# An adapter and expert-FFN kernel: the start of the first adapter, the expert bias fold and the last output stage rearranged

## The chip, the core and the metric

The kernel runs on one core of one Trainium2 chip. A core has five engines that run their own instruction streams side by side and wait for each other through semaphores: TensorE (PE, matrix products into the PSUM memory; its weight loads are listed as PEld), VectorE (DVE), ScalarE (ACT), GpSimd (POOL) and SyncE (SP, which here only issues transfers). Data moves between the device's memory and the on-chip SBUF by 16 DMA engines. The metric is the time of one execution on the device in microseconds; lower is better.

## What is computed

The input x is 2 sequences of 2048 tokens with 512 features, all in 32-bit floats. Two layers follow one another. The first is an adapter with an expert chosen per sequence by `itok_B_0_15`, the second a feed-forward network (FFN) with an expert chosen per sequence by `itok_B_0_7`:

```python
# layer 0: A = 128, 16 experts
hidden = gelu(x @ down_W.T + down_b)
expert_out = hidden @ expert_W[idx].T + expert_b[idx]
domain_output = where(valid, expert_out, hidden)
hidden = domain_output + domain_emb[idx]
hidden = hidden @ up_W.T + up_b
x = layernorm(hidden + x, eps=1e-5) * ln_gamma + ln_beta
# layer 1: I = 2048, 8 experts
h = gelu(x @ Wi[e] + bi[e])
o = h @ Wo[e] + bo[e]
out = layernorm(o + x, eps=1e-12) * gamma[e] + beta[e]
```

## The kernel before

The 4096 tokens are handled as eight blocks of 512 (`TB`), four to a sequence. A block is four subtiles of 128 tokens by 512 features; `x_tiles[n]` holds block n and is changed in place until it is stored. The order of all instructions is written out by hand: each engine runs its instructions in the order in which the program states them, and waits where an operand or a buffer isn't ready.

The loop over n at the end of the program runs `f_in(n)` (the FFN's first matrix with its gelu) and then `f_out(n)` (its second matrix). Both use a Strassen-like scheme that needs seven block products for eight, with sums of weight blocks made by GpSimd (`sums_wi`, `sums_wo`) and sums of activations by VectorE. Products go through `product` (L380) and are called pX, pY, pZ, pW in the first stage and gX, gY, gZ, gW in the second, after their PSUM banks. Other small work is hung between the products by hooks: the adapter of block n + 1 sits in the hooks of `f_out(n)`, the final layernorm of block n - 1 in those of `f_in(n)`, and the loads of later weights too.

For block 0 there is no FFN to hide the adapter in, so it is written out ahead of the loop (L645 to L699), and this is what most of the change touches. Its steps are these.

- `keep_busy(k)` issues k products of a matrix of ones that nobody reads, into the bank called idle. Each 32-bit product shows as two records in the profile.
- `a_transpose(0, s)` transposes subtile s of x on TensorE (pt_x, four pieces) and ScalarE copies it to SBUF as xT. For block 0 the banks are the two of `ps_z`. The matrices down_W and up_W are transposed in the same way and copied by VectorE (dWT, uWT).
- The product pflags spreads the two flags (expert valid or not) over 128 partitions.
- `a_down(0, s, s + 1)` is the down projection of one subtile (pdown), followed by ScalarE's gelu into hid. In block 0 all four use the single bank of `ps_w`.
- `fold_expert` lets VectorE mix the expert's matrix with the identity by the flag (eff), and makes the expert's bias plus the domain embedding into a column, which it spreads to a 128 x 128 tile (biasx). `fold_up` multiplies eff with uWT (pw), and ScalarE copies the result (up): expert and up projection become one matrix.
- `a_up(0, s)` is the up projection of a subtile (pup): hid times up, then `add_bias`, which is biasx times uWT and a one-row product of ones with up_b. VectorE adds the result to x and takes mean and variance; GpSimd makes the inverse deviation (rstd).
- `a_norm(0, s)` normalizes on VectorE in two instructions (L279, L280), `a_out(0, s)` transposes the result for the FFN (pt_y), with ScalarE's copy to yT. `fold_bi` transposes the FFN's first bias.

For the other blocks `fold_bias` makes the whole bias of the up projection once for a sequence (pb, copied by ScalarE to the sequence's upb), and `a_residual(n)` lets GpSimd add it to x ahead of the up projection. The folds of the second sequence are hooked into `f_in(3)`.

Small PSUM tiles come from `aux`, a pool of two banks (`ps_a`) taken in turns: a third tile waits until the first is read.

Transfers at the start go out on two queues. ScalarE issues down_W, two subtiles of x, down_b, up_W, up_b, and the layernorm rows broadcast to 128 partitions (g, b). SyncE issues the token indices, two subtiles of x, and then, when the expert's number has been loaded into a register, the expert's matrix (ew), its bias and the domain embedding as columns (eb), and the FFN's weights.

The last block's `f_out_last` has no hooks. Its two last product pairs are split by subtile (q = 0, 1), Y and V of each in banks of their own; VectorE adds them to x, and the four subtiles are normalized and stored, 2 and 3 first.

Of the kernel before, what the change touches and what calls it, by code (L numbers as in the profile page):

```python
# [9 lines left out]
F32 = mybir.dt.float32  # L10
# [7 lines left out]
def kernel(  # L18
# [34 lines left out]
    P = 128  # L53
# [32 lines left out]
    def aux(name, pool=None, tag="aux"):  # L86
        return (pool or ps_a).tile([P, 512], F32, tag=tag, name=name)
# [24 lines left out]
    db = cpool.tile([A, 1], F32, name="db")  # L112
    g0 = cpool.tile([P, D], F32, name="g0")
    b0 = cpool.tile([P, D], F32, name="b0")
    upb = cpool.tile([1, D], F32, name="upb")
    nc.sync.dma_start(x_tiles[0][:, 0, :], xr[0][:, 0, :])
    nc.scalar.dma_start(dW, down_W)
    nc.sync.dma_start(x_tiles[0][:, 1, :], xr[0][:, 1, :])
# [1 line left out]
    nc.scalar.dma_start(x_tiles[0][:, 3, :], xr[0][:, 3, :])  # L120
    nc.scalar.dma_start(db, down_b.rearrange("(a o) -> a o", o=1))
    nc.scalar.dma_start(uW, up_W.rearrange("(c p) a -> p c a", p=P))
    nc.scalar.dma_start(upb, up_b.rearrange("(o d) -> o d", o=1))
    nc.scalar.dma_start(g0, ln_gamma.partition_broadcast(P))
    nc.scalar.dma_start(b0, ln_beta.partition_broadcast(P))

# [28 lines left out]

    def load_expert(b):
        w = seq[b]
        w["ew"] = spool.tile([A, A], F32, tag="ew", name=f"ew_{b}")
        nc.sync.dma_start(w["ew"], expert_W[ds(e0[b], 1)].rearrange("e o a -> (e o) a"))
        w["eb"] = spool.tile([A, 2], F32, tag="eb", name=f"eb_{b}")  # L160
        nc.sync.dma_start(w["eb"][:, 0:1], expert_b[ds(e0[b], 1)].rearrange("e o -> o e"))
        nc.sync.dma_start(w["eb"][:, 1:2], domain_emb[ds(e0[b], 1)].rearrange("e o -> o e"))

    def load_bi(b):
        w = seq[b]
# [8 lines left out]
    def fold_expert(b):  # L174

        w = seq[b]
        v, iv = flags_all[:, 0, b : b + 1], flags_all[:, 1, b : b + 1]

        eff = spool.tile([A, A], F32, tag="eff", name=f"eff_{b}")
        nc.vector.tensor_scalar(eff, ident, iv, None, ALU.mult)  # L180
        nc.vector.scalar_tensor_tensor(eff, w["ew"], v, eff, ALU.mult, ALU.add)
        bias = spool.tile([A, 1], F32, tag="ebias", name=f"ebias_{b}")
        nc.vector.scalar_tensor_tensor(bias, w["eb"][:, 0:1], v, w["eb"][:, 1:2], ALU.mult, ALU.add)
        biasx = spool.tile([A, P], F32, tag="biasx", name=f"biasx_{b}")
        nc.vector.tensor_scalar(biasx, ones, bias, None, ALU.mult)
        w["biasx"], w["eff"] = biasx, eff

    def fold_up(b):
        w = seq[b]
# [2 lines left out]
        w["up"] = spool.tile([A, D], F32, tag="up", name=f"up_{b}")  # L192
        nc.scalar.copy(w["up"], pw)

    def fold_bias(b):
        w = seq[b]
        pb = aux(f"pb_{b}")
        add_bias(pb, w, True)
        w["upb"] = spool.tile([P, D], F32, tag="upb", name=f"upb_{b}")
        nc.scalar.copy(w["upb"], pb)  # L200

    def add_bias(bank, w, start):

        nc.tensor.matmul(bank, w["biasx"], uWT, start=start, stop=False)
        nc.tensor.matmul(bank, ones[0:1, :], upb, start=False, stop=True)  # L205

    def fold_bi(b):
        w = seq[b]
# [91 lines left out]
    def a_down(n, lo, hi):  # L300

        xT = live["xT"]
        if lo == 0:
            live["hid"] = t_pool.tile([A, TB], F32, tag="hid", name=f"hid_{n}")
        t = slice(lo * P, hi * P)
        ph = aux(f"pdown_{n}_{lo}", ps_w, "W") if n == 0 else aux(f"pdown_{n}")
        for c in range(NC):
            nc.tensor.matmul(ph[:, t], dWT[:, c, :], xT[:, c, t], start=(c == 0), stop=(c == NC - 1))  # L308
        nc.scalar.activation(live["hid"][:, t], ph[:, t], AF.Gelu, bias=db, scale=1.0)

    def a_residual(n):

        for s in range(NS):
            nc.gpsimd.tensor_tensor(x_tiles[n][:, s, :], x_tiles[n][:, s, :], seq[n // BPB]["upb"], ALU.add)

    def a_up(n, s):
        w = seq[n // BPB]
        pu = aux(f"pup_{n}_{s}")
        nc.tensor.matmul(pu, live["hid"][:, ts(s, P)], w["up"], start=True, stop=(n > 0))  # L319
        if n == 0:  # L320
            add_bias(pu, w, False)
        r = x_tiles[n][:, s, :]
        nc.vector.tensor_add(r, pu, r)
        if s == 0:
            live["mv"] = moments_tile(f"a_{n}")
        moments(live["mv"], s, r, f"a_{n}_{s}")
        if n == 0:
            live["rstd", s] = rstds(live["mv"], s, s + 1, EPS0, f"a_{n}_{s}")
        elif s % 2:
            live["rstd", s] = live["rstd", s - 1] = rstds(live["mv"], s - 1, s + 1, EPS0, f"a_{n}_{s}")  # L330
# [181 lines left out]
    def f_out(n, hooks, last):  # L512
# [27 lines left out]
        def f_out_last(n, add):  # L540

            X, Z, W = bank(ps_x, "X"), bank(ps_z, "Z"), bank(ps_w, "W")
            every = range(NP)
            mul(X, a11, w["b11"], early, True)
            h_s13(n, ND - 1)
            h_s2(n, 0)
            h_s2(n, 1)
            mul(X, a11, w["b11"], late, False)
            add(r11, X)
            mul(Z, "s1", w["t1"], every, True)  # L550
            h_s4(n, 0)
            h_s4(n, 1)
            add(r22, Z)
            add(r12, Z)
            mul(X, "s2", w["t2"], every, False)
            add(r12, X)
            mul(X, s3, w["t3"], every, False)
            add(r21, X)
            add(r22, X)
            mul(W, a22, w["t4"], every, True)  # L560
            add(r21, W)
            for s in (2, 3):
                f_moments(n, s)
            f_rstd(n, 2, 4)
            for q in range(2):
                Y, V = (bank(ps_y, "Y"), bank(ps_z, "Z")) if q == 0 else (bank(ps_a, "aux"), bank(ps_a, "aux"))
                mul(Y, a12, w["b21"], every, True, (q,))
                mul(V, "s4", w["b22"], every, True, (q,))
                f_normalize(n, 2 + q)
                f_store(n, 2 + q)  # L570
                add(r11[:, q], Y[:, q])
                add(r12[:, q], V[:, q])
                f_moments(n, q)
                f_rstd(n, q, q + 1)
            for q in range(2):
                f_normalize(n, q)
                f_store(n, q)

        if last:
            f_out_last(n, add)  # L580
# [77 lines left out]
        for _ in range(k):  # L658
            nc.tensor.matmul(idle[:, :P], ones, ones, start=True, stop=True, skip_group_check=True)  # L659

    idle = aux("idle", ps_y, "Y")
    dWT = cpool.tile([P, NC, A], F32, name="dWT")
    uWT = cpool.tile([A, D], F32, name="uWT")
    flags_all = cpool.tile([P, 2, B], F32, name="flags_all")
    keep_busy(24)
    a_transpose(0, 0)
    pd = aux("pt_dW")
    for c in range(NC):
        nc.tensor.transpose(pd[:, ts(c, P)], dW[:, ts(c, P)], ident)
    nc.vector.tensor_copy(dWT.rearrange("p c a -> p (c a)"), pd)  # L670
    a_transpose(0, 1)
    pf = aux("pflags")
    nc.tensor.matmul(pf[:, : 2 * B], ones[0:1, :], flags.rearrange("o f b -> o (f b)"), start=True, stop=True)
    nc.vector.tensor_copy(flags_all.rearrange("p f b -> p (f b)"), pf[:, : 2 * B])
    a_transpose(0, 2)
    a_down(0, 0, 1)
    a_transpose(0, 3)
    pu = aux("pt_uW")
    for c in range(NC):
        nc.tensor.transpose(pu[:, ts(c, P)], uW[:, c, :], ident)  # L680
    nc.vector.tensor_copy(uWT, pu)
    for s in range(1, NS):
        a_down(0, s, s + 1)
    keep_busy(4)
    fold_expert(0)
    fold_up(0)
    a_up(0, 0)
    a_up(0, 1)
    keep_busy(8)
    a_norm(0, 0)  # L690
    fold_bi(0)
    a_norm(0, 1)
# [92 lines left out]
```

## Time and profile before

| what | us |
|---|---|
| median of three runs (lowest, highest) | 903.06 (902.8, 903.95) |
| the profiled execution | 903.51 |
| its span in the profile | 901.7 |

The profile covers one execution. Its span is 1.8 us shorter than that execution's time. A look at the stretches of the span gives this (busy microseconds of each engine):

| stretch, us | what runs | PE | DVE | ACT | POOL | DMA share |
|---|---|---|---|---|---|---|
| 1.06 to 9.36 | idle products | 8.30 | 1.22 | 1.17 | 0.31 | 0.75 |
| 9.36 to 23.19 | transposes, down projections, fold, first up projection | 12.24 | 2.50 | 4.40 | 0.00 | 1.06 |
| 23.19 to 36.35 | other up projections, layernorm | 12.29 | 10.04 | 1.17 | 2.27 | 0.93 |
| 36.35 to 54.21 | first FFN products of block 0 | 17.33 | 10.00 | 4.07 | 17.70 | 0.00 |
| 54.21 to 414.47 | blocks 0 to 2 and the first FFN stage of block 3 | 360.26 | 195.16 | 100.14 | 144.53 | 0.19 |
| 475 to 880 | blocks 4 to 7 | 403.09 | 220.77 | 106.23 | 147.96 | 0.19 |
| 894.1 to 901.7 | after the last product | 0.00 | 4.27 | 0.00 | 0.99 | 0.18 |

A busy TensorE is not a TensorE doing useful work: the idle products count as busy. A line of the timeline reads: start in us, length in us, engine, line, operation, output and input by the program's names, shapes, how many instructions are merged, and in brackets how long the engine stood idle before it and what released it. The chain of waits lists the work that ended last, followed back from the end.

### The profile page before, as it was taken

Reading aid. Unit: us, or ns where it says so; the run is one execution under the profiler, and the core shown is the slowest. Engines: PE = TensorE matmul, PEld = TensorE weight load, DVE = VectorE, ACT = ScalarE, POOL = GpSimd, SP = SyncE. Lnnn points to the kernel's source line nnn. Section 1 sums busy time; section 2 is a strip of 40 time slices with the busy share of each in tenths; the row PEclk is TensorE's granted clock in tenths of the full one; section 3 lists DMA queues with packets and bytes.
Section 4 is the critical chain, followed back from the end, with each engine's and each line's share of the span. In section 5 each row is a group of like instructions: output and inputs, shape, how many; then the busy total and the mean of one; then the engine's idle time right before and its main releaser. Section 6 shows DMA issues by size and latency. Waiting matters only on the chain.

```text
span 901.7 us, 10542 instructions
## 1 busy us (share of the span) xinstructions
PE 888.1 (98%) x4112; PEld 751.3 (83%) x4112; DVE 484.0 (54%) x691; ACT 225.1 (25%) x461; POOL 335.0 (37%) x251
## 2 busy tenths in 40 slices
PE   8999999999999999999999999999999999999996
PEld 7588888887888878888788888888888887888875
DVE  1644374743657546563556747464474853556325
ACT  2134201441024301343013520144101440124200
POOL 0498511542214612344026971144411551223001
PEclk9999999999999999999999999999999999999999
DMA  8522100340013300151007610034000440011001
GB/s 287 218 73 71 45 1 1 128 152 1 1 40 134 108 0 1 63 186 48 0 1 257 187 47 1 0 117 155 10 1 1 140 141 1 1 48 45 1 1 47
DMA packets 47286, 62.16 MB, mean 69 GB/s; under 512 B 2917, under 2 KB 36485, under 8 KB 46342
## 3 DMA queue, kind: packets, MB, share of 16 engines
q1 hardware_dynamic: 45844, 59.93, 19.5%
q10 hardware_dynamic: 1394, 1.58, 0.6%
q8 instruction: 32, 0.52, 0.2%
q14 instruction: 16, 0.13, 0.1%
HBM read 53.11 MB, written 8.39 MB: 68 GB/s over the span
## 4 chain that ended last, share of the span: by engine, by line
PE 98%; DVE 1%; ACT 0%; issue 0%; DVEq 0%
PE gX L380 18%; PE pX L380 18%; PE pZ L380 12%; PE gZ L380 12%; PE gW L380 6%; PE pW L380 6%; PE pY L380 6%; PE gY L380 6%; PE pup L319 3%; PE pdown L308 3%; PE pC L380 2%; PE pt_x L292 2%; PE pt_y L292 1%; PE idle L659 1%; PE gaux L380 1%; PE pup L205 0%
## 5 line engine op out<-in xcount | busy, mean ns | idle before, releaser
L400 ACT ACTIVATE h<-c,biT 128x256 f32<-128x256 f32 x248 | 105.7, 497 | 76.1 <-DVE c L447 76.1
L380 PE MATMUL gX<-wo,h 128*128 128x256 f32 x512 | 115.6, 379 | 1.7 <-DVE x L537 1.7
L380 PE MATMUL pX<-yT,wi 128*128 128x256 f32 x496 | 117.2, 379 | 0.0
L380 PEld LDWEIGHTS gX<-wo,h 128*128 128x128 f32 x512 | 95.6, 190 | 14.1 <-DVE x L537 2.1
L380 PEld LDWEIGHTS pX<-yT,wi 128*128 128x128 f32 x496 | 94.2, 190 | 12.8
L443 ACT COPY c<-pX 128x512 f32<-128x512 f32 x93 | 54.0, 581 | 182.4 <-PE pX L380 182.4
L275 POOL TENSOR_TENSOR rstd_a<-ve_a,mhalf 128x2 f32<-128x2 f32 (+1 forms) x18 | 16.0, 888 | 204.1 <-DVE ve_a L273 204.1
L231 POOL TENSOR_TENSOR wis<-wi 128x512 f32<-128x512 f32 x31 | 40.8, 1315 | 129.5 <-PE pZ L380 129.5
L447 DVE TENSOR_TENSOR c<-pX,c 128x512 f32<-128x512 f32 x31 | 21.4, 691 | 111.2 <-ACT c L443 111.2
L293 ACT COPY yT<-pt_y 128x512 f32<-128x512 f32 x32 | 18.7, 587 | 227.9 <-PE pt_y L292 227.9
L537 DVE TENSOR_TENSOR x<-gX,x 128x512 f32<-128x512 f32 x32 | 21.4, 688 | 99.5 <-PE gX L380 99.4
L275 POOL TENSOR_TENSOR rstd_f<-ve_f,mhalf 128x4 f32<-128x4 f32 (+2 forms) x10 | 10.2, 1025 | 155.6 <-DVE ve_f L273 155.6
L504 DVE TENSOR_TENSOR s<-s,h 128x512 f32<-128x512 f32 x32 | 35.7, 1155 | 47.9 <-PE gZ L380 47.9
L343 POOL TENSOR_TENSOR x<-x,bo 128x512 f32<-128x512 f32 x32 | 41.4, 1298 | 53.2 <-PE pt_y L292 53.2
L380 PEld LDWEIGHTS gX<-wos,s 128*128 128x128 f32 x256 | 48.6, 190 | 13.2 <-issue 6.7
L380 PE MATMUL pX<-yTs,wis 128*128 128x256 f32 x248 | 58.7, 379 | 0.0
L380 PEld LDWEIGHTS gZ<-wos,s 128*128 128x128 f32 x256 | 48.6, 190 | 12.1 <-issue 6.2
L380 PE MATMUL pZ<-yT,wis 128*128 128x256 f32 x248 | 58.6, 379 | 0.0
L380 PE MATMUL pZ<-yTs,wis 128*128 128x256 f32 x248 | 58.6, 379 | 0.0
L380 PE MATMUL pY<-yT,wi 128*128 128x256 f32 x248 | 58.6, 379 | 0.0
L380 PE MATMUL pW<-yTs,wi 128*128 128x256 f32 x248 | 58.6, 379 | 0.0
L380 PE MATMUL gX<-wos,s 128*128 128x256 f32 x256 | 57.8, 379 | 0.3 <-DVE x L537 0.3
(114 smaller groups left out, 1544.8 us busy)
## 6 DMA issues: line engine op xcount, KB each, us to landing
wi<-in_L_cond_Wi_dram SPq DMA_DIRECT2D x64, 512.0 KB, 4.4
wo<-in_L_cond_Wo_dram SPq DMA_DIRECT2D x16, 512.0 KB, 10.2
out_dram<-x SPq DMA_DIRECT2D x32, 256.0 KB, 2.0
x<-in_x_dram SPq DMA_DIRECT2D x7, 1024.0 KB, 6.4
x<-in_x_dram SPq DMA_DIRECT2D x2, 256.0 KB, 4.6
x<-in_x_dram ACTq DMA_DIRECT2D x2, 256.0 KB, 4.7
bo<-in_L_cond_bo_dram SPq DMA_DIRECT2D x2, 256.0 KB, 5.3
gamma<-in_L_cond_gamma_dram SPq DMA_DIRECT2D x2, 256.0 KB, 6.8
```

What stands on the lines that cost most here:

```text
L231: tt(s1, a21, a22, ALU.add)
L275: nc.gpsimd.tensor_tensor(rstd[:, lo:hi], ve[:, lo:hi], mhalf[:, lo:hi], ALU.pow)
L292: nc.tensor.transpose(pt[:, ts(c, P)], src[:, ts(c, P)], ident)
L308: nc.tensor.matmul(ph[:, t], dWT[:, c, :], xT[:, c, t], start=(c == 0), stop=(c == NC - 1))
L319: nc.tensor.matmul(pu, live["hid"][:, ts(s, P)], w["up"], start=True, stop=(n > 0))
L343: nc.gpsimd.tensor_tensor(r, r, seq[n // BPB]["bo"], ALU.add)
L380: nc.tensor.matmul(bank[:, q], lhsT(k, q), rhs(k, q), start=first, stop=True, skip_group_check=True)
L400: nc.scalar.activation(h[:, j, c * HT : (c + 1) * HT], pre[:, q], AF.Gelu, bias=w["bi"][:, j : j + 1], scale=1.0)
L443: nc.scalar.copy(t, src)
L447: nc.vector.tensor_add(t, src, t)
L504: nc.vector.tensor_tensor(t[:, i : i + 2], s1[:, i : i + 2], h_blocks(n, k, k + 2)[0], ALU.subtract)
L537: nc.vector.tensor_add(t, src, t)
```

## The change

There are six parts.

1. Idle products: 9 instead of 24 at the start, and none of the 4 and 8 later ones. They use a bank of `ps_x` instead of the one of `ps_y`.
2. Order at the start: flags and down_W's transposes go ahead of the transposes of x; all four transposes of x then go ahead of the down projections. Those alternate between the banks of `ps_w` and `ps_y`. The fold of the expert (`fold_expert`, `fold_up`) moves ahead of the last down projection.
3. The expert's bias: expert_b and domain_emb are loaded as rows, ahead of the expert's matrix. VectorE makes their sum as a row, and a small product of that row with a row of ones (pe) gives biasx, which ScalarE copies out of PSUM. This holds for both sequences.
4. up_b is loaded broadcast to 128 partitions.
5. GpSimd adds it to the four subtiles of block 0 (`a_residual(0)`), and the one-row product with up_b leaves block 0's up projections. `fold_bias` keeps it.
6. In `f_out_last` subtile 0 is normalized and stored between the two last adds, ahead of the add of the last product.

```diff
--- before.py
+++ after.py
@@ -112,7 +112,7 @@
     db = cpool.tile([A, 1], F32, name="db")
     g0 = cpool.tile([P, D], F32, name="g0")
     b0 = cpool.tile([P, D], F32, name="b0")
-    upb = cpool.tile([1, D], F32, name="upb")
+    upb = cpool.tile([P, D], F32, name="upb")
     nc.sync.dma_start(x_tiles[0][:, 0, :], xr[0][:, 0, :])
     nc.scalar.dma_start(dW, down_W)
     nc.sync.dma_start(x_tiles[0][:, 1, :], xr[0][:, 1, :])
@@ -120,7 +120,7 @@
     nc.scalar.dma_start(x_tiles[0][:, 3, :], xr[0][:, 3, :])
     nc.scalar.dma_start(db, down_b.rearrange("(a o) -> a o", o=1))
     nc.scalar.dma_start(uW, up_W.rearrange("(c p) a -> p c a", p=P))
-    nc.scalar.dma_start(upb, up_b.rearrange("(o d) -> o d", o=1))
+    nc.scalar.dma_start(upb, up_b.partition_broadcast(P))
     nc.scalar.dma_start(g0, ln_gamma.partition_broadcast(P))
     nc.scalar.dma_start(b0, ln_beta.partition_broadcast(P))
 
@@ -155,11 +155,11 @@
 
     def load_expert(b):
         w = seq[b]
+        w["eb"] = spool.tile([1, 2, A], F32, tag="eb", name=f"eb_{b}")
+        nc.sync.dma_start(w["eb"][:, 0, :], expert_b[ds(e0[b], 1)])
+        nc.sync.dma_start(w["eb"][:, 1, :], domain_emb[ds(e0[b], 1)])
         w["ew"] = spool.tile([A, A], F32, tag="ew", name=f"ew_{b}")
         nc.sync.dma_start(w["ew"], expert_W[ds(e0[b], 1)].rearrange("e o a -> (e o) a"))
-        w["eb"] = spool.tile([A, 2], F32, tag="eb", name=f"eb_{b}")
-        nc.sync.dma_start(w["eb"][:, 0:1], expert_b[ds(e0[b], 1)].rearrange("e o -> o e"))
-        nc.sync.dma_start(w["eb"][:, 1:2], domain_emb[ds(e0[b], 1)].rearrange("e o -> o e"))
 
     def load_bi(b):
         w = seq[b]
@@ -175,15 +175,13 @@
 
         w = seq[b]
         v, iv = flags_all[:, 0, b : b + 1], flags_all[:, 1, b : b + 1]
+        row = spool.tile([1, A], F32, tag="ebias", name=f"ebias_{b}")
+        nc.vector.scalar_tensor_tensor(row, w["eb"][:, 0, :], flags[:, 0, b : b + 1], w["eb"][:, 1, :], ALU.mult, ALU.add)
 
         eff = spool.tile([A, A], F32, tag="eff", name=f"eff_{b}")
         nc.vector.tensor_scalar(eff, ident, iv, None, ALU.mult)
         nc.vector.scalar_tensor_tensor(eff, w["ew"], v, eff, ALU.mult, ALU.add)
-        bias = spool.tile([A, 1], F32, tag="ebias", name=f"ebias_{b}")
-        nc.vector.scalar_tensor_tensor(bias, w["eb"][:, 0:1], v, w["eb"][:, 1:2], ALU.mult, ALU.add)
-        biasx = spool.tile([A, P], F32, tag="biasx", name=f"biasx_{b}")
-        nc.vector.tensor_scalar(biasx, ones, bias, None, ALU.mult)
-        w["biasx"], w["eff"] = biasx, eff
+        w["ebias"], w["eff"] = row, eff
 
     def fold_up(b):
         w = seq[b]
@@ -192,17 +190,18 @@
         w["up"] = spool.tile([A, D], F32, tag="up", name=f"up_{b}")
         nc.scalar.copy(w["up"], pw)
 
+        pe = aux(f"pe_{b}")
+        nc.tensor.matmul(pe[:, :P], w["ebias"], ones[0:1, :], start=True, stop=True)
+        w["biasx"] = spool.tile([A, P], F32, tag="biasx", name=f"biasx_{b}")
+        nc.scalar.copy(w["biasx"], pe[:, :P])
+
     def fold_bias(b):
         w = seq[b]
         pb = aux(f"pb_{b}")
-        add_bias(pb, w, True)
+        nc.tensor.matmul(pb, w["biasx"], uWT, start=True, stop=False)
+        nc.tensor.matmul(pb, ones[0:1, :], upb[0:1, :], start=False, stop=True)
         w["upb"] = spool.tile([P, D], F32, tag="upb", name=f"upb_{b}")
         nc.scalar.copy(w["upb"], pb)
-
-    def add_bias(bank, w, start):
-
-        nc.tensor.matmul(bank, w["biasx"], uWT, start=start, stop=False)
-        nc.tensor.matmul(bank, ones[0:1, :], upb, start=False, stop=True)
 
     def fold_bi(b):
         w = seq[b]
@@ -303,22 +302,27 @@
         if lo == 0:
             live["hid"] = t_pool.tile([A, TB], F32, tag="hid", name=f"hid_{n}")
         t = slice(lo * P, hi * P)
-        ph = aux(f"pdown_{n}_{lo}", ps_w, "W") if n == 0 else aux(f"pdown_{n}")
+        if n == 0:
+            ph = aux(f"pdown_{n}_{lo}", *((ps_y, "Y") if lo % 2 else (ps_w, "W")))
+        else:
+            ph = aux(f"pdown_{n}")
         for c in range(NC):
             nc.tensor.matmul(ph[:, t], dWT[:, c, :], xT[:, c, t], start=(c == 0), stop=(c == NC - 1))
         nc.scalar.activation(live["hid"][:, t], ph[:, t], AF.Gelu, bias=db, scale=1.0)
 
     def a_residual(n):
 
+
+        by = seq[n // BPB]["upb"] if n else upb
         for s in range(NS):
-            nc.gpsimd.tensor_tensor(x_tiles[n][:, s, :], x_tiles[n][:, s, :], seq[n // BPB]["upb"], ALU.add)
+            nc.gpsimd.tensor_tensor(x_tiles[n][:, s, :], x_tiles[n][:, s, :], by, ALU.add)
 
     def a_up(n, s):
         w = seq[n // BPB]
         pu = aux(f"pup_{n}_{s}")
         nc.tensor.matmul(pu, live["hid"][:, ts(s, P)], w["up"], start=True, stop=(n > 0))
         if n == 0:
-            add_bias(pu, w, False)
+            nc.tensor.matmul(pu, w["biasx"], uWT, start=False, stop=True)
         r = x_tiles[n][:, s, :]
         nc.vector.tensor_add(r, pu, r)
         if s == 0:
@@ -562,19 +566,24 @@
             for s in (2, 3):
                 f_moments(n, s)
             f_rstd(n, 2, 4)
-            for q in range(2):
-                Y, V = (bank(ps_y, "Y"), bank(ps_z, "Z")) if q == 0 else (bank(ps_a, "aux"), bank(ps_a, "aux"))
+            banks = (bank(ps_y, "Y"), bank(ps_z, "Z")), (bank(ps_a, "aux"), bank(ps_a, "aux"))
+            for q, (Y, V) in enumerate(banks):
                 mul(Y, a12, w["b21"], every, True, (q,))
                 mul(V, "s4", w["b22"], every, True, (q,))
-                f_normalize(n, 2 + q)
-                f_store(n, 2 + q)
+
+            def finish(s):
+                f_normalize(n, s)
+                f_store(n, s)
+
+            for q, (Y, V) in enumerate(banks):
+                finish(2 + q)
                 add(r11[:, q], Y[:, q])
+                if q:
+                    finish(0)
                 add(r12[:, q], V[:, q])
                 f_moments(n, q)
                 f_rstd(n, q, q + 1)
-            for q in range(2):
-                f_normalize(n, q)
-                f_store(n, q)
+            finish(1)
 
         if last:
             f_out_last(n, add)
@@ -658,35 +667,33 @@
         for _ in range(k):
             nc.tensor.matmul(idle[:, :P], ones, ones, start=True, stop=True, skip_group_check=True)
 
-    idle = aux("idle", ps_y, "Y")
+    idle = aux("idle", ps_x, "X")
     dWT = cpool.tile([P, NC, A], F32, name="dWT")
     uWT = cpool.tile([A, D], F32, name="uWT")
     flags_all = cpool.tile([P, 2, B], F32, name="flags_all")
-    keep_busy(24)
-    a_transpose(0, 0)
+    keep_busy(9)
+    pf = aux("pflags")
+    nc.tensor.matmul(pf[:, : 2 * B], ones[0:1, :], flags.rearrange("o f b -> o (f b)"), start=True, stop=True)
+    nc.vector.tensor_copy(flags_all.rearrange("p f b -> p (f b)"), pf[:, : 2 * B])
     pd = aux("pt_dW")
     for c in range(NC):
         nc.tensor.transpose(pd[:, ts(c, P)], dW[:, ts(c, P)], ident)
     nc.vector.tensor_copy(dWT.rearrange("p c a -> p (c a)"), pd)
-    a_transpose(0, 1)
-    pf = aux("pflags")
-    nc.tensor.matmul(pf[:, : 2 * B], ones[0:1, :], flags.rearrange("o f b -> o (f b)"), start=True, stop=True)
-    nc.vector.tensor_copy(flags_all.rearrange("p f b -> p (f b)"), pf[:, : 2 * B])
-    a_transpose(0, 2)
+    for s in range(NS):
+        a_transpose(0, s)
+    a_residual(0)
     a_down(0, 0, 1)
-    a_transpose(0, 3)
+    a_down(0, 1, 2)
     pu = aux("pt_uW")
     for c in range(NC):
         nc.tensor.transpose(pu[:, ts(c, P)], uW[:, c, :], ident)
     nc.vector.tensor_copy(uWT, pu)
-    for s in range(1, NS):
-        a_down(0, s, s + 1)
-    keep_busy(4)
+    a_down(0, 2, 3)
     fold_expert(0)
     fold_up(0)
+    a_down(0, 3, 4)
     a_up(0, 0)
     a_up(0, 1)
-    keep_busy(8)
     a_norm(0, 0)
     fold_bi(0)
     a_norm(0, 1)
```

## The prediction

> **What bounds the kernel now.** I read the page first, then the chain of waits in order of time, then the timeline of the first 60 us and of the last 20.
>
> ```profile
> span 901.7 us, 10542 instructions
> PE 888.1 (98%) x4112; PEld 751.3 (83%) x4112; DVE 484.0 (54%) x691; ACT 225.1 (25%) x461; POOL 335.0 (37%) x251
> PE 98%; DVE 1%; ACT 0%; issue 0%; DVEq 0%
> ```
>
> TensorE is busy all the time and carries the chain, so no other engine's work in the middle is worth anything. But "busy" in the first 36 us includes filler. The chain there, piece by piece (start, length, what):
>
> ```profile
> 1.06 8.57 PE idle L659 x48
> ...
> 17.73 0.89 PE idle L659 x8
> 18.62 0.88 PE pw L191 x2
> ...
> 19.52 0.59 ACT up L193
> ...
> 20.16 1.13 PE pup L319 x2
> 21.28 0.86 PE pup L204 x2
> 22.14 1.05 PE pup L205 x2
> 23.19 1.06 PE pup L319 x2
> ...
> 26.16 1.98 PE idle L659 x16
> ```
>
> Idle products hold 8.57 + 0.89 + 1.98 = 11.4 us of chain. Each up projection is three matmuls, about 2.97 us, for four subtiles; the third (L205) multiplies one row of ones by the up bias. At 36.35 the first FFN product (pC) starts, and from there to 880 TensorE hardly waits. Call T the end of the first up projection (23.19); T to pC is 13.16 us.
>
> The end, from the timeline:
>
> ```profile
> 890.64 0.42 DVE L537 TENSOR_TENSOR x<-gaux,x 128x256 f32<-128x256 f32 x1 [0.45 <-PE gaux L380]
> 894.10 0.43 DVE L537 TENSOR_TENSOR x<-gaux,x 128x256 f32<-128x256 f32 x1 [3.03 <-PE gaux L380]
> ...
> 895.50 0.15 DVE L273 TENSOR_SCALAR ve_f<-mv_f 128x1 f32<-128x1 f32 x1
> 895.57 0.74 DVE L279 SCALAR_TENSOR_TENSOR x<-x,mv_f,gamma 128x512 f32<-128x512 f32 x1
> 895.74 0.99 POOL L275 TENSOR_TENSOR rstd_f<-ve_f,mhalf 128x1 f32<-128x1 f32 x1 [5.92 <-DVE ve_f L273]
> 896.42 0.75 DVE L280 SCALAR_TENSOR_TENSOR x<-x,rstd_f,beta 128x512 f32<-128x512 f32 x1
> 897.09 0.74 DVE L279 SCALAR_TENSOR_TENSOR x<-x,mv_f,gamma 128x512 f32<-128x512 f32 x1
> 897.93 0.75 DVE L280 SCALAR_TENSOR_TENSOR x<-x,rstd_f,beta 128x512 f32<-128x512 f32 x1
> ```
>
> VectorE normalizes two subtiles after the last matmul, although the first was ready before a 3.03 us idle.
>
> **What the Trainium skill says.** "TensorE: Matmul & The Clock Gate", What's actually happening: the array starts at half rate and goes to full rate after about 3.4 us of sustained work, counted in a free-running window. The trace agrees in kind: idle products start every 0.213 us until about 6.8 us and every 0.107 after, though it took 5.7 us. "SBUF — State Buffer", Who interferes with whom: a VectorE instruction with two SBUF inputs and a GpSimd one that reads SBUF block each other whole. The trace agrees: the normalize step at L279 takes 0.74 us alone (27.94) and 1.75 at 37.52 beside GpSimd's sums (L231, 1.60 there, 1.27 elsewhere). "TensorEngine Tiling (Array Packing)", Key Properties: a change of tiling mode drains the array. I read the one-row products so: L205 takes 1.05 against 0.86 for L204, and the product after it 1.06 against 0.86, 0.19 us at each edge.
>
> **The change part by part.**
>
> *Start, to the fold.* Nine products instead of 24: 18 records at 0.213 from 1.06 end near 4.9. The flags product (flags ready at 3.71 + 0.16 = 3.87) then waits for nothing: to 5.4. The dW transposes (dW lands at 1.07 + 2.8 = 3.9) take 4 x 0.213: to 6.25; VectorE's copy (0.69) ends at 7.05. x: the second subtile lands at 1.86 + 4.6 = 6.5, the first, issued 0.4 us earlier, near 6.1, the last ACT one at 7.3 (4.7 is the mean of 4.1 and 5.3, issue 2.00). So the transposes of x follow at once, and TensorE works without a gap until about 7: I take the clock to rise at 6.8 as before. They go through two Z banks and ScalarE copies of 0.59, so ScalarE sets the pace: copies end at 7.7, 8.3, 9.0, 9.65, TensorE is through at 8.95. Down projections at 0.89: 0 to 9.8, 1 (now in the Y bank, so it no longer waits for gelu 0) to 10.7, uW transposes 0.44 to 11.1, uWT copied at 11.85, down 2 to 12.0.
>
> The fold on VectorE: row about 0.2 (0.21 for the bias column now), eff 0.28 + 0.35, without hindrance at about 12.65. Its inputs: on SP, ew moves behind two row loads; slots were 6.14, 6.69, 7.21, so ew goes out at 7.2 and, with the 3.8 us it had (the wait of the bi load on ew ended at 10.0), lands at 11.0. The wi, bi and bo loads behind it keep their slots. eb as rows goes out at 6.14 and 6.69; columns landed in 3.5 and 4.9 us, so rows by 10.2 to 11.6 at worst.
>
> Hindrance: GpSimd now adds up_b to the four subtiles. upb grows from 2 KB to 256 KB; its issue stays at 4.95 and g right behind it landed 4.3 us after its own, so I take 9.4. Then four adds of 1.27 to 1.7 us run from 9.4 to about 15, over the fold. Row and the second eff step have two SBUF inputs; each may wait for the rest of one add (0 to 1.27). I take 1.25 in all: eff at 13.9. pw 0.88 to 14.85, up copied (0.59) at 15.45; the new product pe (two records of 128 columns, 0.21, plus 0.19 at its edges) to 15.25, biasx copied (0.37) at 15.8, both beside down 3 (0.89 + 0.19, to 16.35). Up projection 0: 2 x 0.86, so T = 18.05 instead of 23.19: **5.15 saved**. That down 3 now lies behind the fold is what hides the copies; without it they would cost about 0.6.
>
> upb's extra 254 KB take 0.7 us at 348 GB/s (9.36 to 23.19). It delays g (landed 9.8, read at T + 3.6), wi, wo and x1 by as much; wo is first read by GpSimd's sums (L255) at 49. Hidden.
>
> *T to pC.* The one-row products go: 4 x 1.25 (0.86 + two edges) and 1.98 of filler leave TensorE. What is late next is VectorE, in program order after T: up 0 with statistics 1.86, up 1 1.74, two normalizes and the biT copy 3.19 (27.94 to 31.13), up 2 1.9, up 3's add 0.74: T + 9.4, and the last transposes, ScalarE's copy and pC's start 1.38 more (34.97 to 36.35). TensorE fits in between, also with two aux banks (up 3 waits for biT's bank until T + 5.3, ends T + 7.1). pC at T + 10.8: **2.36 saved**. GpSimd's rstd stays hidden behind the other normalize; the residual adds are over by 15, before the first add on VectorE.
>
> *pC to 880.* Nothing goes or comes except, at the second sequence's fold (403), pe: 0.21 + 2 x 0.19: **0.6 lost**, between 0.3 (no edges) and 0.9 (the bias product behind it then waits for the biasx copy; queued behind it are all FFN products). ScalarE would copy biasx at 405.2 to 405.6, and the bias product is due at 406.2, so no wait. VectorE's shorter fold there (0.29 for biasx) was hidden anyway.
>
> *End.* Normalize and store of subtile 0 (1.5 us) go between the two last adds, into the 3.03 us idle: 891.1 to 892.7. SP's stores keep order, one goes earlier. After the last matmul the remaining normalize's second half waits for GpSimd's rstd (895.74 + 0.99), so it starts at 896.8 and ends at 897.55 instead of 898.68: **1.13 saved**. At worst 0.75 if the wait costs more, at best 1.5 with the last store running alone.
>
> Sum: 5.15 + 2.36 - 0.6 + 1.13 = 8.0. Against its own time the profiled execution goes from 903.51 (span 901.7 and 1.8 around it) to 895.5; the median shown is 0.45 lower, so 903.06 becomes **895.0**.
>
> **Rivals.**
>
> *No collision.* The adds fall elsewhere, or the 128-column steps slip between them: 1.25 more, 893.7. For it: the two steps are short. Against it: four adds back to back cover 5.6 us around the fold.
>
> *A later fold.* Each VectorE step waits out a full add (up to 2.5), or ew or the eb rows land 1 to 2 us later because upb shares the DMA engines, whose share was already 0.97 to 1.08 between 3 and 7 us; or the clock rises one window (3.4 us) later, which costs the down projections 0.9 each. About 2.5 lost: 897.5. Against it: 3 us lie between ew's landing and its use.
>
> *Cold array (slower).* With the filler gone, TensorE has gaps before x and between banks, and no window counts as busy until the FFN starts. Then records double: down 0 to 2 2.7, x transposes 0.65, uW, pw, pe and down 3 2.6, up 0 1.72, so 7.7 to T; the stage after T becomes TensorE's, 2.3; pC's first windows 2.6. That is 12.6: 907.6. It decides once the array stays at half rate past T (7.7 plus some of the 2.3 eats the 8.0). Against it: TensorE is gapless to about 7 us and some 80% busy to the fold; gaps after it are about 1 us.
>
> **How the numbers follow.** The forecast's own range is 893.8 to 896.8; chance 0.50. No collision 0.19, later fold 0.24, cold 0.05; 0.02 for no change, which only a partly cold array could make. Range 892.8 to 898.2: below it a better end, above it the cold case and part of the later fold. Faster by over 0.2% (1.8 us, about what a measurement of this kernel can tell) 0.93, same 0.02, slower 0.05.
>
> **What would show it.** T near 18 and pC near 29; idle records spaced 0.213 until the flags product and transposes at 0.107 from about 7; GpSimd's adds between 9 and 15 and VectorE's eff step lengthened beside them; the VectorE-bound stretch of 10.8 after T; the product behind pe lengthened by 0.19 near 395; the last VectorE step starting right after GpSimd's rstd. The prediction is wrong if 512-column records show about 0.85 instead of 0.43 before pC, if the eff step ends after 16, or if pC waits for wi.

## The result and the profile after

| | median, us | lowest to highest | runs |
|---|---|---|---|
| before | 903.06 | 902.65 to 904.04 | 7 |
| changed | 899.22 | 895.56 to 902.11 | 7 |

The ratio is 0.9948 with a 95% interval of 0.9926 to 0.9971. The change gains 3.8 us, about half a per cent, where 8.0 were forecast, and its runs spread over 6.5 us where those of before spread over 1.4. The profiled execution is the slowest of the seven, 902.11, only 1.40 below that of before. The page of the changed kernel (span; busy time of the engines; chain by engine):

```profile
span 900.3 us, 10433 instructions
PE 883.6 (98%) x4054; PEld 747.2 (83%) x4054; DVE 485.0 (54%) x689; ACT 225.3 (25%) x463; POOL 339.7 (38%) x255
PE 94%; DVE 1%; issue 1%; ACT 0%; POOLq 0%; POOL 0%; DVEq 0%; ACTq 0%
```

TensorE has 58 records fewer, but only 4.5 us less busy time; part of what was taken away came back as slower products. The timeline shows where it begins:

```profile
12.01 5.09 POOL L318 TENSOR_TENSOR x<-x,upb 128x512 f32<-128x512 f32 x4 [10.64 <-DMA eb<-n_L_cond_domain_emb_dram]
...
12.85 0.57 DVE L179 SCALAR_TENSOR_TENSOR ebias<-eb,flags 1x128 f32<-1x128 f32 x1
...
13.35 1.34 DVE L182 TENSOR_SCALAR eff<-ident,flags_all 128x128 f32<-128x128 f32 x1
14.73 1.25 DVE L183 SCALAR_TENSOR_TENSOR eff<-ew,flags_all,eff 128x128 f32<-128x128 f32 x1
...
16.04 1.12 PE L189 MATMUL pw<-uWT,eff 128*128 128x512 f32 x2 [2.94 <-DVE eff L183]
...
19.67 1.92 PE L323 MATMUL pup<-up,hid 128*128 128x512 f32 x2
```

The label in brackets names the load of eb; upb itself landed at 11.9 (issued at 5.49, 6.4 us to landing). GpSimd's four adds lie over the fold on VectorE, whose two eff steps take 1.34 and 1.25 us. In the kernel before:

```profile
14.25 0.28 DVE L180 TENSOR_SCALAR eff<-ident,flags_all 128x128 f32<-128x128 f32 x1
...
14.56 0.35 DVE L181 SCALAR_TENSOR_TENSOR eff<-ew,flags_all,eff 128x128 f32<-128x128 f32 x1
```

TensorE stands idle 2.94 us for eff, and the first up projection's pair of records then takes 1.92 us against 1.13 before. The same in a table by stretches (length; busy time and number of instructions of PE, PEld, DVE, ACT, POOL; granted TensorE clock; DMA share; GB/s):

```profile
13.00:16.00 3.00, 0.10 (x1) 0.00 (x0) 2.95 (x3) 0.37 (x1) 3.00 (x4) 1.00 1.09 360
...
17.00:24.00 7.00, 7.00 (x17) 4.10 (x17) 0.60 (x1) 1.22 (x3) 0.10 (x1) 0.51 1.08 362
...
34.00:38.00 4.00, 4.00 (x12) 3.21 (x12) 3.79 (x4) 0.00 (x0) 3.92 (x3) 0.57 0.67 259
```

The third number from the end is the one to see: after three microseconds with almost no matmul TensorE runs at half rate for seven, and once more at the start of the FFN. The kernel before in the same stretches:

```profile
13.00:16.00 3.00, 2.54 (x22) 2.27 (x20) 1.65 (x5) 1.09 (x3) 0.00 (x0) 1.00 1.10 356
...
17.00:24.00 7.00, 6.33 (x25) 3.11 (x24) 0.73 (x2) 0.95 (x2) 0.00 (x0) 1.00 1.07 375
...
34.00:38.00 4.00, 3.13 (x17) 2.31 (x17) 3.52 (x7) 1.17 (x2) 1.83 (x2) 1.00 0.25 96
```

(The column reads 1.00 in the first microseconds too, where the idle records are spaced 0.213 us; it does not show that slow start.) The seven timed runs, each with its mean granted clock, follow the same order:

| us | 895.56 | 895.60 | 898.45 | 899.22 | 899.63 | 899.74 | 902.11 |
|---|---|---|---|---|---|---|---|
| clock | 0.999 | 0.999 | 0.997 | 0.997 | 0.997 | 0.995 | 0.993 |

One stretch of 3.4 us at half rate takes 1.7 of 900 us from the mean clock, 0.002; the profiled run had three such lengths (6.83 from 17.14 on and 3.42 from 34.20). The clock also falls behind the last product, where nothing is left for TensorE to do (from 897.8 on here, from 898.1 in the kernel before). How much of that lies inside the span moves the mean by up to about 0.002 as well, so the row gives an order and not a count of stretches.

The second sequence's fold, from the chain of waits in order of time, and the end from the timeline:

```profile
402.19 0.86 PE pw L189 x2
403.05 0.41 PE pe L194 x2
403.47 1.92 PE pZ L384 x8
```

```profile
890.41 0.42 DVE L541 TENSOR_TENSOR x<-gaux,x 128x256 f32<-128x256 f32 x1 [0.45 <-PE gaux L384]
890.75 0.74 DVE L278 SCALAR_TENSOR_TENSOR x<-x,mv_f,gamma 128x512 f32<-128x512 f32 x1
891.60 0.75 DVE L279 SCALAR_TENSOR_TENSOR x<-x,rstd_f,beta 128x512 f32<-128x512 f32 x1
893.87 0.42 DVE L541 TENSOR_TENSOR x<-gaux,x 128x256 f32<-128x256 f32 x1 [1.51 <-PE gaux L384]
...
895.50 0.99 POOL L274 TENSOR_TENSOR rstd_f<-ve_f,mhalf 128x1 f32<-128x1 f32 x1 [5.92 <-DVE ve_f L272]
896.53 0.75 DVE L279 SCALAR_TENSOR_TENSOR x<-x,rstd_f,beta 128x512 f32<-128x512 f32 x1 [0.44 <-POOL rstd_f L274]
```

Subtile 0 is normalized in the idle stretch between the last adds, and one step is left behind GpSimd's rstd.

### The profile page after: what moved, and what is told of

It reads as the page before. It is cut to its first block, busy times and chain, and to the rows that moved or that the text cites. A ratio compares the mean times of both kernels' runs of the same rounds, so it can differ in the third digit from the quotient of the medians.

```text
span 900.3 us, 10433 instructions
## 1 busy us (share of the span) xinstructions
PE 883.6 (98%) x4054; PEld 747.2 (83%) x4054; DVE 485.0 (54%) x689; ACT 225.3 (25%) x463; POOL 339.7 (38%) x255
## 4 chain that ended last, share of the span: by engine, by line
PE 94%; DVE 1%; issue 1%; ACT 0%; POOLq 0%; POOL 0%; DVEq 0%; ACTq 0%
PE gX L384 18%; PE pX L384 18%; PE pZ L384 12%; PE gZ L384 12%; PE gW L384 6%; PE pW L384 6%; PE pY L384 6%; PE gY L384 6%; PE pdown L310 3%; PE pup L323 3%; PE pC L384 2%; PE pt_y L291 2%; PE pt_x L291 1%; DVE x L541 0%; DVE x L279 0%
## 5 line engine op out<-in xcount | busy, mean ns | idle before, releaser
L384 PEld LDWEIGHTS gX<-wo,h 128*128 128x128 f32 x512 | 95.6, 190 | 14.1 <-DVE x L541 2.1
L292 ACT COPY yT<-pt_y 128x512 f32<-128x512 f32 x32 | 18.7, 587 | 225.2 <-PE pt_y L291 225.2
L384 PEld LDWEIGHTS gX<-wos,s 128*128 128x128 f32 x256 | 48.6, 190 | 13.2 <-issue 6.7
L384 PEld LDWEIGHTS gZ<-wos,s 128*128 128x128 f32 x256 | 48.6, 190 | 12.1 <-issue 6.2
```

The source lines that it names most:

```text
L384: nc.tensor.matmul(bank[:, q], lhsT(k, q), rhs(k, q), start=first, stop=True, skip_group_check=True)
```

## The experiments

Two theories stood against each other. The clock theory: the gap ahead of pw makes the clock fall, and that is the larger loss. The collision theory: VectorE's wait for GpSimd is the loss, the clock a side show. All comparisons are with runs of the kernel before on the same chip (their median was 902.91 to 903.49).

### e1_fill: idle products in the gap

```diff
+    keep_busy(14)
     fold_expert(0)
     fold_up(0)
```

> The changed kernel with 14 idle products (28 records, 3.0 us at full rate) between the third down projection and the fold product pw, where TensorE stood idle 2.9 us for eff. Clock theory (that idle stretch makes a clock window count as idle, and the array runs at half rate for two windows, 17.1 to 23.9 in the profiled run): eff still ends near 16, but the 512-column records after it start every 0.43 us and not 0.85, T is near 20.2 instead of 23.4, pC starts near 30.7, and the time is 896 to 897.5 with a spread of under 1.5 us between runs. Collision theory (only VectorE's wait for GpSimd's adds costs, the clock is a side show): T stays above 22.5, the time stays at 899 or rises with the filler.

Measured: 896.80 (896.70 to 897.15), ratio 0.9924 (0.9907 to 0.9940). Its stretches and the end of the gap:

```profile
13.00:16.00 3.00, 2.69 (x25) 2.50 (x23) 2.93 (x3) 0.00 (x0) 2.81 (x3) 1.00 1.10 349
...
17.00:24.00 7.00, 6.27 (x23) 3.31 (x23) 3.32 (x9) 1.12 (x3) 0.55 (x1) 1.00 1.07 367
```

```profile
16.02 1.12 PE L189 MATMUL pw<-uWT,eff 128*128 128x512 f32 x2 [0.33 <-DVE eff L183]
...
30.53 7.17 PE L384 MATMUL pC<-yT,wi 128*128 128x256 f32 x32 [0.68 <-ACT yT L292]
```

pw starts at the same time as in the profiled run of the change, but the clock stays at 1.00, T (the end of the first up projection) is 20.4 and not 23.36, and pC takes 7.17 us and not 8.87. Twenty-eight records that nobody reads take 2.4 us off the median and shrink the spread from 6.5 us (seven runs) to 0.45 (four). The clock theory holds; the collision, untouched here, still costs its part.

### e2_adds_after_fold: the adds wait for eff

```diff
-    a_residual(0)
...
     fold_expert(0)
+    gate = small.tile([P, 1], F32, tag="gate", name="gate")
+    nc.gpsimd.tensor_tensor(gate, seq[0]["eff"][:, 0:1], seq[0]["eff"][:, 0:1], ALU.add)
+    a_residual(0)
     fold_up(0)
```

> The changed kernel with GpSimd's four adds of the up bias held back until eff is done (a one-column GpSimd add reads eff first). Both theories: the row and both eff steps fall back to about 0.2, 0.28 and 0.35 us; eff then ends at 14.5, where ew (landed at 14.1 in the profiled run) sets it. Clock theory: TensorE's gap ahead of pw shrinks from 2.9 to about 1.5 us, the clock mostly holds, T is near 18.7, pC near 29.2, time near 895. Collision theory: only the 1.5 us of eff come back, so T near 21.9, 897.7.

Measured: 894.70 (894.47 to 895.18), ratio 0.9901 (0.9885 to 0.9918). The timeline:

```profile
12.76 0.33 DVE L179 SCALAR_TENSOR_TENSOR ebias<-eb,flags 1x128 f32<-1x128 f32 x1
13.02 0.27 DVE L182 TENSOR_SCALAR eff<-ident,flags_all 128x128 f32<-128x128 f32 x1
...
13.32 0.35 DVE L183 SCALAR_TENSOR_TENSOR eff<-ew,flags_all,eff 128x128 f32<-128x128 f32 x1
...
13.73 1.12 PE L189 MATMUL pw<-uWT,eff 128*128 128x512 f32 x2 [0.72 <-DVE eff L183]
...
13.90 4.93 POOL L318 TENSOR_TENSOR x<-x,upb 128x512 f32<-128x512 f32 x4
```

The fold steps are short again, TensorE waits 0.72 us and no stretch ahead of the last product is below full clock; pC starts at 28.24. The adds run from 13.9 to 18.8, and the first one is done well before VectorE's first add at 18.18. Against e1, whose adds still meet the fold, the median is 2.1 us lower, about what eff is earlier (16.0 to 13.7, 2.3 us). So the collision costs 2.1 to 2.3 us by itself, and opens the gap that costs the rest.

### e3_product_bias: the adds and the broadcast undone

```diff
-    upb = cpool.tile([P, D], F32, name="upb")
+    upb = cpool.tile([1, D], F32, name="upb")
...
-    nc.scalar.dma_start(upb, up_b.partition_broadcast(P))
+    nc.scalar.dma_start(upb, up_b.rearrange("(o d) -> o d", o=1))
...
-            nc.tensor.matmul(pu, w["biasx"], uWT, start=False, stop=True)
+            nc.tensor.matmul(pu, w["biasx"], uWT, start=False, stop=False)
+            nc.tensor.matmul(pu, ones[0:1, :], upb[0:1, :], start=False, stop=True)
...
-    a_residual(0)
```

> The changed kernel with its parts 4 and 5 undone: up_b is loaded as one row again, no adds by GpSimd in block 0, the one-row product back in the four up projections; all else as changed. If the adds are what spoils the start: eff ends by 14 (256 KB less ahead of ew), TensorE's gap is near 1 us, the clock holds, an up projection takes 2.97 us again, T near 19.5, pC near 31.5 (TensorE-bound: three more up projections of 2.97 and the transposes), time 896 to 897, less than the whole change. If the start is lost for another reason (ScalarE's late copies of xT, ew's landing), it comes out slower than the whole change, near 900 to 901, as the product adds 4 x 1.25 us to TensorE.

Measured: 898.16 (897.52 to 898.81), ratio 0.9937 (0.9920 to 0.9953), over a microsecond more than expected. The start is better than expected (eff at 13.2, T at 18.7, pC at 30.51), but in the profiled run, 898.81, pC went cold (it ran at half rate):

```profile
30.51 8.86 PE L385 MATMUL pC<-yT,wi 128*128 128x256 f32 x32 [0.67 <-ACT yT L292]
```

That costs 1.7 us in this run. It is not the whole miss: two of the four runs took 897.52 and 897.62 with a mean clock of 0.999, which leaves no room for such a stretch, and they too lie 0.5 us or more above the expected 897. That part is not explained. The stretch ahead of pC (24.0 to 30.5 in the profiled run) shows TensorE 5.64 us busy of 6.5, more than e1's 4.22, whose pC stayed at full rate. So the busy share of the trace alone doesn't tell whether the clock falls, and a short gap ahead of pw (0.72 us here) doesn't keep it up all the way to the FFN.

### e4_tail_only: the last stage alone

The edit is the change's own to `f_out_last`, on the kernel before.

> The kernel before with part 6 alone: subtile 0 normalized and stored between the two last adds. From the trace of the changed kernel (VectorE ends 3.4 us after the last product instead of 4.6): 1.17 us saved, 901.9, with the rest of the span as before. If the store of the last subtile overlapped something in the kernel before, 0.8 or less is left.

Measured: 901.99 (20 runs) against 903.49 (23 runs), ratio 0.9984 (0.9977 to 0.9991), a gain of 0.8 to 2.1 us. The forecast 1.13 lies in it.

### e5_loads_moved and e6_own_banks: toward a better start

On top of e2, e5 moves the two layernorm rows to the other queue and the expert's matrix ahead of its rows (only the first is printed here):

```diff
-    nc.scalar.dma_start(g0, ln_gamma.partition_broadcast(P))
-    nc.scalar.dma_start(b0, ln_beta.partition_broadcast(P))
...
     load_expert(0)
+    nc.sync.dma_start(g0, ln_gamma.partition_broadcast(P))
+    nc.sync.dma_start(b0, ln_beta.partition_broadcast(P))
     load_wi(0, 0)
```

> The kernel with the adds after the fold (e2), and besides the g and b rows issued by SyncE behind the expert's loads and not by ScalarE, and the expert's matrix loaded ahead of its two rows again. In e2 ScalarE's first copy of xT starts at 8.1, 0.9 us after its transposes, and the profile names a load as what held it. If that is the issue of the last row load on ScalarE's own queue, the copies start near 7.2 here, the fold ends near 12.7 instead of 13.7, pC starts near 27.3 instead of 28.2, and the time is 893.8. If the copies wait for the data of x or a bank instead, nothing moves: 894.7. If ew or g now come later on the busy DMA engines, eff or the first normalize slips and it is slower than e2.

Measured: 893.79 (893.26 to 894.48), ratio 0.9900 (0.9883 to 0.9916). In the profile ScalarE's copies start at 6.35 and not 8.10 and pC at 26.66 and not 28.24. Against e2's ratio the time can't be told apart; the profile agrees with the expectation, the runs don't settle it. e6 adds banks:

```diff
-        transpose_subtile(x_tiles[n][:, s, :], live["yT"], s, f"y_{n}_{s}")
+        transpose_subtile(x_tiles[n][:, s, :], live["yT"], s, f"y_{n}_{s}", n == 0 and s < 2)
...
-        pt = aux(f"pt_bi_{b}")
+        pt = aux(f"pt_bi_{b}") if b else aux(f"pt_bi_{b}", ps_w, "W")
...
     a_out(0, 0)
+    keep_busy(3)
     a_out(0, 1)
+    keep_busy(3)
```

> e5, and besides: the transposes of the FFN bias and of the first two normalized subtiles get banks outside the pair that the up projections take turns in (the fourth up projection waited for VectorE's copy of the bias, the second transpose for ScalarE's copy of the first), with three idle products ahead of the second transpose and three behind it, where TensorE waits anyway. If the banks set the stretch from T to pC, it shrinks from 10.5 to about 8.5 us (pC then follows VectorE's second normalize), 2 us less than e5, near 892. If VectorE's own order sets it whatever the banks, it stays at 10.5 and the time is that of e5. If the array goes cold in the sparser stretch, pC takes 8.9 us and not 7.2 and 1.7 us of it are lost again.

Measured: 892.21 (891.94 to 893.08), ratio 0.9878 (0.9862 to 0.9895), the fastest version here and ahead of both kernels. Its timeline ahead of pC, TensorE only:

```profile
22.76 1.02 PE L323 MATMUL pup<-uWT,biasx 128*128 128x512 f32 x2
23.62 0.60 PE L289 MATMUL pt_y<-ident,x 128*128 128x128 f32 x4
24.05 0.83 PE L668 MATMUL idle<-ones 128*128 128x128 f32 x6
25.11 0.66 PE L289 MATMUL pt_y<-ident,x 128*128 128x128 f32 x4 [0.23 <-DVE x L277]
25.61 0.83 PE L668 MATMUL idle<-ones 128*128 128x128 f32 x6
26.44 0.92 PE L382 MATMUL pC<-yT,wi 128*128 128x256 f32 x3
```

The second transpose waits for VectorE's normalize and no longer for a bank, and pC, which takes 7.17 us in all, stays at full rate. VectorE's first add starts at 18.38, so T is 18.3, and T to pC is 8.1 us (10.46 in the changed kernel). In this execution the x transposes waited until 8.1 for data, so it shows less of e5's gain. Banks and idle products were changed together; which of them gives how much was not tried.

### e7_fewer_idle_only: part 1 alone on the kernel before

```diff
-    keep_busy(24)
+    keep_busy(9)
...
-    keep_busy(4)
...
-    keep_busy(8)
```

> The kernel before with part 1 alone: 9 idle products at the start instead of 24, none of the 4 and 8 later. Nothing else changed. Clock theory: TensorE gets gaps (ahead of x's first subtile, in the down projections that wait for gelu, behind up projections), some windows count as idle, and the spread between runs grows to 2 us or more; the removed filler of 0.89 + 1.98 plus some 2.5 us of the first is partly eaten: 898 to 901. If filler only costs and the clock is a side show: 902.9 less 5 us, 898, with a spread as before.

Measured: 898.76 (898.39 to 899.01), ratio 0.9953 (0.9936 to 0.9970). The spread is 0.6 us, and between the start and the last product the profile shows no stretch at half rate: here the clock theory's expectation of a spread failed, only the size is within it. In the old order the small products lie closer, with 2.19 us of TensorE work between 13 and 16 where the change has 0.10. Part 1 alone gives what the whole change gives (0.9948): with the collision and the cold stretches, the other five parts together add nothing that shows.

### e8_upb_early: the broadcast bias sent earlier

```diff
     nc.sync.dma_start(x_tiles[0][:, 1, :], xr[0][:, 1, :])
+    nc.sync.dma_start(upb, up_b.partition_broadcast(P))
...
-    nc.scalar.dma_start(upb, up_b.partition_broadcast(P))
```

> The changed kernel with the broadcast up bias issued by SyncE behind its second subtile of x (near 2.3 us) and not by ScalarE at 5.5; the adds are not held back. If it is the meeting of the adds with the fold that opens TensorE's gap, the time of upb's landing decides: it lands near 8 and not at 11.9, the adds run from 8 to 13, at most the last of them meets the fold, eff ends near 13.5, no cold stretch ahead of T, 895. If the 256 KB ahead of x, uW and ew on the DMA engines cost as much, the transposes of x start 0.7 us later or more, and it stays at 896.5 or above. If the clock falls whatever the fold does, 898 to 899 as the whole change.

Measured: 895.30 (894.99 to 897.01), ratio 0.9917 (0.9901 to 0.9934). The adds run from 8.26 to 13.2, eff ends at 14.05, TensorE waits 0.72 us, T is 18.5. The transposes of x waited 0.54 us for data. Without any gate, moving one load removes the collision in the profiled execution. One of the four runs took 897.01 with a mean clock of 0.997, the others about 895.2 with 0.999; that is near the price of one half-rate stretch, but this run was not profiled.

### The changed kernel three times more

> The changed kernel once more, for a second profile of it. Clock theory: the time is between 895.5 and 902; if it is under 897, no 512-column record before pC takes 0.85 us and pC takes 7.2 us; if it is near 899, one of the two cold stretches shows; VectorE's fold steps are lengthened by the adds in every case.

> The changed kernel once more, to see what an execution near 895.6 has that those near 899 lack. Clock theory alone: the same fold (eff near 16) without a cold window, which by the filler's run is 896.8 and not 895.6. Clock and loads: upb lands at another time, so that the adds meet the fold less, eff ends before 15, and the gap is too short for a cold window.

> As the third: one of two outcomes. Under 896.5: eff before 15 and no cold window. Near 899: eff near 16 and one cold window, or two cold windows near 900.

They took 898.80, 897.14 and 897.21. after_again had eff at 16 and one half-rate stretch (17.5 to 20.9). after_third had eff at 16 and none: T 20.4, as in e1. after_fourth had an early upb and a cold stretch, one at half rate, all the same:

```profile
8.86 5.07 POOL L318 TENSOR_TENSOR x<-x,upb 128x512 f32<-128x512 f32 x4 [7.49 <-DMA upb<-in_L_cond_up_b_dram]
...
12.40 0.33 DVE L179 SCALAR_TENSOR_TENSOR ebias<-eb,flags 1x128 f32<-1x128 f32 x1
12.66 1.34 DVE L182 TENSOR_SCALAR eff<-ident,flags_all 128x128 f32<-128x128 f32 x1
14.04 0.35 DVE L183 SCALAR_TENSOR_TENSOR eff<-ew,flags_all,eff 128x128 f32<-128x128 f32 x1
14.44 1.12 PE L189 MATMUL pw<-uWT,eff 128*128 128x512 f32 x2 [1.80 <-DVE eff L183]
...
17.78 1.81 PE L323 MATMUL pup<-up,hid 128*128 128x512 f32 x2
```

Only the last add meets the fold, so eff ends at 14.4; but the clock fell behind a gap of 1.80 us (0.50 between 16 and 17). The expectation for after_fourth named two outcomes, under 896.5 or near 899, and neither came: it had tied the cold stretch to the late fold. So two things vary from one execution to the next, each on its own: when upb lands (adds from 8.86, 10.75, 10.77 and 12.01 in four profiles) and whether a clock stretch falls. Without the late fold and without the cold stretch these two come near 895.5, the two best runs; that those had just this was not profiled.

## Why the prediction was wrong

By its own steps, predicted against the profiled run:

| step | predicted | measured |
|---|---|---|
| last copy of xT | 9.65 | 10.6 |
| upb landed, adds start | 9.4 | 12.0 |
| uWT copied | 11.85 | 12.93 |
| eff | 13.9 | 15.98 |
| pw's start to T | 4.1 | 7.3 |
| T to pC | 10.8 | 10.46 |
| pC (as before) | 7.17 | 8.87 |
| second fold | 0.6 lost | 0.60 lost |
| end | 1.13 saved | 1.17 saved |

The step that failed is "Start, to the fold", which gave "T = 18.05 instead of 23.19: 5.15 saved"; T was 23.36. Two of its terms were wrong.

The first is a size. "Row and the second eff step have two SBUF inputs; each may wait for the rest of one add ... I take 1.25 in all." The collision came, but the first eff step, with one SBUF input, waited as well (1.34 us, 0.27 in e2): the three steps took 3.2 us, in e2 0.95. Between e1 and e2 eff moves by 2.3 us, so the collision was undersized by about 1.05. The other half is the chain ahead of the fold: ScalarE's copies of xT began at 8.20, behind the issue of b's load on its own queue (7.79 to 8.15), where the prediction let them begin when the transposes were done. In e2, without a collision, eff ended at 13.67 and not at the 12.65 of "without hindrance", 1.0 late; e5, which takes the two loads off that queue, has eff at 12.1. Together that is the 2.1 us by which eff was late.

The second is a missing term. The prediction used the clock for the start alone: "I take the clock to rise at 6.8 as before". Its own numbers had down 2 ending at 12.0 and pw starting near 13.95, a gap of 2 us (the rivals speak of gaps of "about 1 us") made wider by every microsecond of the collision, and no term for what the gap does to the clock. It stood only in rivals, as a later rise or as an array cold all the way to the FFN. What happened lies between: the clock rose, fell behind the gap and rose again. From pw to T it took 7.3 us against 4.1 predicted; e1, which changes nothing but the gap, gives 4.4, and so does the changed kernel itself in after_third, without a cold stretch. So 2.9 of the 3.2 us are the clock and 0.3 an undersized chain. pC lost 1.7 more. From the forecast 8.05 this leaves 8.05 - 2.1 - 3.2 + 0.3 - 1.7 = 1.35 (the 0.3 is the shorter stretch from T to pC), and 1.40 was measured. That is the slowest of the seven runs; the median is 2.9 us lower, and its mean clock higher (0.997 against 0.993). One of the prediction's own signs of being wrong came: 512-column records 0.85 us apart before pC.

The page of the Trainium skill that the prediction used for the rise, "TensorE: Matmul & The Clock Gate", What's actually happening, tells of the fall too: the clock goes back to half after an idle window of about 3.4 us. The half-rate stretches agree with that length (6.83 is twice, 3.42 once), but no full window of idleness was needed: in the 3.41 us before the fall, from 13.73 to 17.14, TensorE was 1.10 us busy.

Right were the edges of the one-row products, the fold of the second sequence and the end. The stretch from T to pC came out near its forecast too, 10.46 against 10.8, but not for the reason given: the prediction put the shared banks at nothing ("TensorE fits in between, also with two aux banks"), and in e6, with banks of their own and six idle products, it is 8.1 us. That the adds lie over the fold was right by luck: upb was expected at 9.4 and landed at 11.9, and from both times on the adds reach the fold. In after_fourth, with the adds from 8.86, the collision lengthened one step by 1.07 us, near the 1.25 forecast; with the adds from 10.7 on or later (e1 and the three other profiles of the changed kernel) all three steps were lengthened. The rival "a later fold" named two of the causes and its 897.5 is near the runs at 897 to 899; the cold array to the slower side was the right mechanism for the wrong length.

## What to carry to other kernels

Filler on TensorE may hold the clock up for what follows: before taking it out, list the gaps that remain and price each with the half-rate work behind it. Taken out alone it cost nothing here (e7); with a late fold behind it, it did. Work moved to GpSimd isn't free because GpSimd is idle; look for what VectorE does at that time, and let a dependency or an earlier load put it elsewhere. Where a changed kernel's runs spread more than those of before, look at each run's granted clock before explaining the median, and leave out of it what falls behind the last product.

## What was not expected of the hardware

Loads that broadcast one 2 KB row to 128 partitions landed late and at uneven times. In the changed kernel (issue, size, us to landing):

```profile
upb<-in_L_cond_up_b_dram ACTq DMA_DIRECT2D x1, 256.0 KB, 6.4
g<-in_L_cond_ln_gamma_dram ACTq DMA_DIRECT2D x1, 256.0 KB, 7.4
...
ew<-in_L_cond_expert_W_dram SPq DMA_DIRECT2D x1, 64.0 KB, 6.3
```

dW, a plain load of the same size and the first large one, took 2.9 us, the two pairs of x 4.0 and 5.1. In after_fourth upb took 3.7, in after_again and after_third 5.5 and 5.6. From 9 to 10 us the DMA engines were busy throughout (share 1.04) and moved 63 GB/s, and the expert's matrix issued at 7.79 landed at 14.1. Which of the loads then in flight is slow, and why, was not tried.

A VectorE step that multiplies one SBUF tile by a scalar for each partition (128x128, 0.27 us) took 1.34 beside GpSimd's adds, as long as one add (1.27) and a little more.

The falls of the clock lie on a grid. In the changed kernel's profile it falls at 17.14, at 34.20 and, behind the last product, at 897.78: 5 and 258 steps of 3.413 us after the first. after_again (falls at 17.48 and 894.71), after_fourth (15.94 and 893.17) and e3 (30.99 and 894.56) fit the same step, each with the grid in another place. So the same gap meets the grid differently in each execution. after_third, whose clock did not fall ahead of the last product, had a gap of 3.07 us ahead of pw, longer than the 2.94 of the profiled run; counted back from its fall at 892.15, a step of the grid ended inside that gap, at 14.92.

How much work keeps the clock up was left open. In the grid step from 14.07 to 17.48 of after_again TensorE was 1.46 us busy, and the clock fell; in that from 11.51 to 14.92 of after_third it was 1.45, and the clock stayed. In e3 it fell behind a step (27.57 to 30.99) with 2.55 us busy.
